# A graph-attention kernel on one core: the work after its last search, laid out in another order and on other engines

## The chip, the core and the metric

The kernel runs on one core of a Trainium2 chip. The core has five engines that each work through their own list of instructions in order: TensorE (PE in the profile; PEld is its loading of weights), VectorE (DVE), ScalarE (ACT), GpSimd (POOL) and SyncE (SP), which here only issues DMAs. They wait for each other by semaphores. 16 DMA engines move data between the chip's memory and the core's own memory. The metric is the time of one execution on the device, in microseconds; lower is better.

## What is computed

The reference is a graph-attention layer with four heads, a residual and a layer norm, over 4096 nodes with 512 features:

```python
ht = (h @ W).reshape(N, N_HEADS, N_HIDDEN).transpose(1, 0, 2)
src = jnp.einsum('hnd,hd->hn', ht, a_src)
dst = jnp.einsum('hnd,hd->hn', ht, a_dst)
e = jax.nn.leaky_relu(src[:, :, None] + dst[:, None, :], SLOPE) + adj_mat[None]
att = jax.nn.softmax(e, axis=-1)
h_prime = jnp.einsum('hij,hjd->hid', att, ht)
return h_prime.mean(axis=0)
...
x = _layernorm(x + _L0_gnn_ref(x, adj, L0_gnn_W, L0_gnn_a), axis=-1)
```

The matrix `adj` (4096 x 4096, 64 MB in fp32) holds values up to 1e9, so in nearly every row one entry is so much larger than all others that the softmax is 1 there and 0 elsewhere. The output row is then the layer norm of x plus one row of x times the mean of W over the heads. The kernel computes this, and tests for every row that the gap to the second largest entry is large enough; where it is not, a general path (a branch that is not taken with these inputs) computes the row in full.

## The kernel before

The 4096 rows are worked on in 32 blocks of 128 (`NB` = 32, row p*32 + ib belongs to block ib). `hold` is a tile with all x rows, block by block; a block's result is written over it and stored from there. The numbers that the text uses: `LATE` = 28 (the last four blocks), `BEHIND` = 24 (the four before them), `Q` = 4, `KB` = 4 pieces of 128 along the 512 features.

The main loop (L400 to L441) takes one block t of `adj` in each pass, while earlier blocks are at later stages:

- `load_adj(t + 5)` issues the DMA of a later block on SyncE; for blocks 28 to 31 in four pieces.
- `segment_maxima` (L158, VectorE) reduces each row's 4096 entries to 64 maxima of segments of 64.
- `find_segment(t)` finds the largest segment (VectorE), computes its address (GpSimd, `row`), and gathers that segment by an indirect DMA that GpSimd issues (`lead`).
- `find_column(t - 2)` finds the place in the segment (VectorE, `within`), computes the column (GpSimd, `col`) and gathers that row of x (`y`, an indirect DMA of GpSimd).
- `turn(t - 3)` transposes the gathered rows on TensorE (4 transposes) and copies the result out of PSUM on ScalarE (`yt`). `residual` starts a PSUM tile with x by a product with the identity, and `products` adds yt times the mean of W, two matmuls for each of four kb (L221).
- `stats(t - 4)` sums and squares the block on ScalarE, `rstd` makes the factor on GpSimd, and `finish` normalises on ScalarE (L261). `row_norm` (L228) sums the squares of x for the test.

Blocks 24 to 27 have no place for their x until then: the rows of `hold` from 16 on held W first, and x of 24 to 31 is loaded only after the last of `adj`. Their products leave PSUM by `put_by` (L234, a ScalarE copy into a free buffer), and x is added later by `add_x` (L237, VectorE).

The last block is searched over its whole row of 4096 (`find_column_in_row`, L201), so that its column is known without a second gather. After the loop comes the drain (L443 to L492), an order written out by hand: every engine takes its instructions in the order of these lines. In it are the x loads of blocks 24 to 31, twelve stores of blocks 0 to 23, the last searches, the row norms, the adding, statistics and normalising of blocks 24 to 31, the test with its three parts (`bound`: the maximum of the row norms, turned by TensorE to one partition, reduced, and spread again by a matmul; `test`: six small VectorE operations; `count`: a matmul that counts, and `report`), and the last stores. Blocks 28 to 30 go through `finish_last` (VectorE adds x to the products, takes `bn_stats` and `bn_aggr`, ScalarE the square root, VectorE the reciprocal and the normalising), block 31 through `finish_in_halves`, the same on two PSUM tiles of 256 columns; `rstd_late` makes the factors of blocks 26 and 27 on VectorE and ScalarE.

PSUM tiles named `o` come from four buffers in turn, tiles `y` from four, `yt` from two.

Of the kernel before, what the change touches and what calls it, by code (L numbers as in the profile page):

```python
# [13 lines left out]
OP = mybir.AluOpType  # L14
# [52 lines left out]
def leading_rows(ctx, tc, x, adj, W, a, out, ident, v, n_bad, any_bad):  # L67
# [47 lines left out]
    def load_x(lo, n):  # L115
        nc.sync.dma_start(hold[:, ds(lo, n), :], x_rows[:, ds(lo, n), :])
# [46 lines left out]
    def find_segment(ib):  # L163
        seg = seg_of.pop(ib)
        nc.vector.max(out=top[:, ib, :], in_=seg)
        at = small.tile([P, 8], U32, name="at")
        nc.vector.max_index(at, top[:, ib, :], seg)  # L167
        row = small.tile([P, 1], U32, name="row")
        nc.gpsimd.tensor_tensor(row, at[:, 0:1], first[:, ib : ib + 1], op=OP.add)  # L169
        lead = small.tile([P, E], F32, name="lead", bufs=2 * Q + 1)  # L170
        nc.gpsimd.indirect_dma_start(  # L171
            out=lead, out_offset=None, in_=adj_segs,
            in_offset=bass.IndirectOffsetOnAxis(ap=row[:, :1], axis=0),
        )
        start = at_of[ib] = small.tile([P, 1], U32, name="start")
        nc.gpsimd.tensor_tensor(start, at[:, 0:1], width, op=OP.mult)
        lead_of[ib] = lead
# [8 lines left out]
    def find_inner(ib):  # L186
        nc.vector.max(out=inner[:, ib, :], in_=lead_of[ib])

    def find_column(ib):
        if ib < BEHIND:  # L190
            find_inner(ib)
        within = small.tile([P, 8], U32, name="within")
        nc.vector.max_index(within, top[:, ib, :], lead_of[ib])  # L193
        col = small.tile([P, 1], U32, name="col")
        nc.gpsimd.tensor_tensor(col, at_of.pop(ib), within[:, 0:1], op=OP.add)  # L195
        gather_rows(ib, col)

    def find_column_in_row(ib):

        col = small.tile([P, 8], U32, name="col")  # L200
        nc.vector.max_index(col, top[:, ib, :], adj_t[ib])  # L201
        gather_rows(ib, col)

    def turn(ib):
        y = y_t.pop(ib)
        tp = psum.tile([P, KB, P], F32, name="tp", bufs=2)
        for kb in range(KB):
            nc.tensor.transpose(tp[:, kb, :], y[:, ts(kb, P)], ident)  # L208
        yt = yt_of[ib] = rows.tile([P, KB, P], F32, name="yt")
        nc.scalar.copy(yt, tp)  # L210
# [5 lines left out]
    def products(ib, lo=0, hi=KB):  # L216
        start = ib not in o_ps
        if start:
            o_ps[ib] = psum.tile([P, D], F32, name="o")
        for kb in range(lo, hi):  # L220
            nc.tensor.matmul(  # L221
                o_ps[ib], yt_of[ib][:, kb, :], w_sum[:, kb, :],
                start=(start and kb == 0), stop=(kb == KB - 1),
            )

    def row_norm(ib):
        sq = rows.tile([P, D], F32, name="sq")
        nc.scalar.activation(sq, hold[:, ib, :], AF.Square, accum_out=xx[:, ib : ib + 1])  # L228
# [4 lines left out]
            o_ps["by"] = adj_pool.tile([P, N // D, D], F32, name="adj_t")  # L233
        nc.scalar.copy(o_ps["by"][:, ib - BEHIND, :], o_ps.pop(ib))  # L234

    def add_x(ib):
        nc.vector.tensor_add(hold[:, ib, :], hold[:, ib, :], o_ps["by"][:, ib - BEHIND, :])  # L237
        o_ps[ib] = hold[:, ib, :]

    def stats(ib):  # L240
# [6 lines left out]
    def rstd(i):  # L247
        nc.gpsimd.tensor_scalar(sd[:, i], sd[:, i], 1.0 / D, EPS, op0=OP.mult, op1=OP.add)
        nc.gpsimd.tensor_tensor(sd[:, i], sd[:, i], power[:, : i.stop - i.start], op=OP.pow)
        nc.gpsimd.tensor_mul(nm[:, i], nm[:, i], sd[:, i])  # L250

    def rstd_late(i):

        nc.vector.tensor_scalar(sd[:, i], sd[:, i], 1.0 / D, EPS, op0=OP.mult, op1=OP.add)
        nc.scalar.activation(sd[:, i], sd[:, i], AF.Sqrt)
        nc.vector.reciprocal(sd[:, i], sd[:, i])
        nc.vector.tensor_mul(nm[:, i], nm[:, i], sd[:, i])

    def finish(ib):
        i = slice(ib, ib + 1)  # L260
        nc.scalar.activation(hold[:, ib, :], o_ps.pop(ib), AF.Identity, bias=nm[:, i], scale=sd[:, i])  # L261
# [10 lines left out]
                start=False, stop=(kb == KB - 1),  # L272
            )

    def finish_in_halves(ib):
        halves = o_ps.pop(ib)
        st = small.tile([P, 2, nc.vector.BN_STATS_DIM], F32, name="st2", bufs=1)
        for k in range(2):
            nc.vector.bn_stats(st[:, k, :], halves[k])
        mv = small.tile([P, nc.vector.BN_AGGR_DIM], F32, name="mv", bufs=2)  # L280
        nc.vector.bn_aggr(mv, st)
        r = small.tile([P, 1], F32, name="r", bufs=2)
        nc.scalar.activation(r, mv[:, 1:2], AF.Sqrt, bias=eps)
        nc.vector.reciprocal(r, r)
        for k in range(2):
            nc.vector.tensor_scalar(
                hold[:, ib, ts(k, D // 2)], halves[k], mv[:, 0:1], r, op0=OP.subtract, op1=OP.mult
            )

    def finish_last(ib, residual):  # L290

        o = o_ps.pop(ib)
        if residual:
            nc.vector.tensor_add(hold[:, ib, :], o, hold[:, ib, :])
            o = hold[:, ib, :]
        st = small.tile([P, nc.vector.BN_STATS_DIM], F32, name="st", bufs=2)
        nc.vector.bn_stats(st, o)
        mv = small.tile([P, nc.vector.BN_AGGR_DIM], F32, name="mv", bufs=2)
        nc.vector.bn_aggr(mv, st)
        r = small.tile([P, 1], F32, name="r", bufs=2)  # L300
        nc.scalar.activation(r, mv[:, 1:2], AF.Sqrt, bias=eps)
        nc.vector.reciprocal(r, r)
        nc.vector.tensor_scalar(hold[:, ib, :], o, mv[:, 0:1], r, op0=OP.subtract, op1=OP.mult)

    def store(queue, lo, n):
        queue.dma_start(out_rows[:, ds(lo, n), :], hold[:, ds(lo, n), :])
# [93 lines left out]
    for t in range(NB):  # L400
        if t == NB // 2:
            tc.mark_branch_hint_location("general", engines=HINTED)
        if t in x_at:
            load_x(*x_at[t])
        load_adj(t + AHEAD)
        middle = 1 if t > LATE else 2
        segment_maxima(t, 0, middle)
        if t >= COLUMN:
            find_column(t - COLUMN)
        segment_maxima(t, middle, PIECES)  # L410
        pair = FINISH <= t < BEHIND + FINISH and t % 2 == 0
        if pair:
            rstd(slice(t - FINISH, t - FINISH + 2))
        find_segment(t)
        if t < 2:
            mean_of_heads(t)
        elif t == 2:
            mean_of_heads(2)
            mean_of_heads(3)
        if t == 0:  # L420
            turn_a()
        turned = [(*vectors[0], turn_w(*vectors.pop(0))) for _ in range(vectors_at.get(t, 0))]
        if t == 16:
            head_norms()
        ib = t - PROJECT
        if ib >= 0:
            turn(ib)
            if ib < BEHIND:
                residual(ib)
        for some in turned:  # L430
            head_vector(*some)
        if ib >= 0:
            products(ib)
        if t >= BEHIND + STATS:
            put_by(t - STATS)
        elif t >= STATS:
            stats(t - STATS)
            row_norm(t - STATS)
        if pair:
            finish(t - FINISH)  # L440
            finish(t - FINISH + 1)  # L441

    for ib in range(BEHIND, NB, 2):  # L443
        load_x(ib, 2)
    for ib in range(0, BEHIND, 2):
        store(nc.sync, ib, 2)
    find_column(NB - 2)
    find_column_in_row(NB - 1)
    for ib in range(BEHIND, NB - 2):
        row_norm(ib)  # L450
    turn(NB - 3)
    for ib in range(NB - 2, NB):
        row_norm(ib)
    products(NB - 3, 0, KB - 1)
    finish_last(NB - 4, True)
    bound(0)
    turn(NB - 2)
    add_x(BEHIND)
    add_x(BEHIND + 1)
    products(NB - 3, KB - 1, KB)  # L460
    residual_in_halves(NB - 1)
    products(NB - 2, 0, 1)
    bound(1)
    products(NB - 2, 1, KB - 1)
    add_x(BEHIND + 2)
    add_x(BEHIND + 3)
    stats(BEHIND)
    stats(BEHIND + 1)
    rstd(slice(BEHIND, BEHIND + 2))
    for ib in range(BEHIND, NB):  # L470
        find_inner(ib)
    bound(2)
    test()
    pg = count()
    stats(BEHIND + 2)
    turn(NB - 1)
    finish_last(NB - 3, True)
    report(pg)
    finish(BEHIND)
    finish(BEHIND + 1)  # L480
    stats(BEHIND + 3)
    products(NB - 2, KB - 1, KB)
    products_of_half(NB - 1, 0)
    products_of_half(NB - 1, 1)
    rstd_late(slice(BEHIND + 2, LATE))
    finish_last(NB - 2, True)
    finish(BEHIND + 2)
    finish(BEHIND + 3)
    for ib, n in ((NB - 4, 1), (NB - 3, 1), (BEHIND, 2), (NB - 2, 1), (BEHIND + 2, 2)):
        store(nc.sync, ib, n)  # L490
    finish_in_halves(NB - 1)
    store(nc.sync, NB - 1, 1)  # L492


# [151 lines left out]
```

## Time and profile before

| | |
|---|---|
| time, median of 5 runs | 245.47 us (243.63 to 245.83) |
| time of the profiled execution | 244.77 us |
| span of the profiled execution, first to last instruction | 243.2 us |
| PE busy | 199.5 us, 82% |
| DVE busy | 189.1 us, 78% |
| ACT busy | 112.2 us, 46% |
| POOL busy | 95.9 us, 39% |
| DMA moved | 97.73 MB, 402 GB/s on average |

Busy time is an average over the whole span. What counts for the end is which wait ends last in the drain, so the profile is read there in order of time. The two lines of the page's DMA part show how the bytes divide, between DMAs that SyncE issues (q1) and the gathers that GpSimd issues (q0); columns are packets, MB and the share of 16 engines' span:

```profile
q1 hardware_dynamic: 11376, 88.09, 87.6%
q0 software_dynamic: 3584, 9.44, 9.9%
```

### The profile page before, as it was taken

To read this page: it belongs to the slowest core of one execution; us is meant where nothing else is said; L and a number is where in the kernel's file an instruction comes from. 1 tells how busy PE (TensorE), PEld (TensorE's weight loads), DVE (VectorE), ACT (ScalarE), POOL (GpSimd) and SP (SyncE) were. 2 spreads that over 40 slices of the span, in tenths; PEclk is the share of its full clock that TensorE was granted. 3 is DMA by queue.
4 is the path that set the end of the run, shared out by engine and by line. 5 is a ranking of instruction groups with operands and counts; after the bars stand their busy time and mean duration, and the time that the engine had idled before them with its cause. 6 is when DMAs were issued, how large, how long until landed. Compare 5 with 4: busy or idle time off the path is not lost.

```text
span 243.2 us, 2510 instructions
## 1 busy us (share of the span) xinstructions
PE 199.5 (82%) x679; PEld 102.9 (42%) x679; DVE 189.1 (78%) x312; ACT 112.2 (46%) x270; POOL 95.9 (39%) x209
## 2 busy tenths in 40 slices
PE   0098959999999999999959779499959888769950
PEld 0034515655555555555324334144424444324530
DVE  2625885499789886999589969895999999986753
ACT  2003002155757575757636455238533851364961
POOL 1012232426435542645254636463556474441100
PEclk9999778999999999999999999979997999997996
DMA  6999999999999999999999999999999999999944
GB/s 238 416 414 424 422 424 426 418 428 412 424 418 421 411 442 413 424 412 430 424 417 416 429 420 424 408 425 424 428 418 398 408 406 409 407 407 418 409 186 175
DMA packets 14993, 97.73 MB, mean 402 GB/s; under 512 B 2296, under 2 KB 2296, under 8 KB 10240
## 3 DMA queue, kind: packets, MB, share of 16 engines
q1 hardware_dynamic: 11376, 88.09, 87.6%
q0 software_dynamic: 3584, 9.44, 9.9%
q8 instruction: 6, 0.10, 0.2%
q14 instruction: 11, 0.09, 0.1%
q10 hardware_dynamic: 16, 0.02, 0.0%
HBM read 89.15 MB, written 8.39 MB: 401 GB/s over the span
## 4 chain that ended last, share of the span: by engine, by line


## 5 line engine op out<-in xcount | busy, mean ns | idle before, releaser
L158 DVE TENSOR_REDUCE seg<-adj_t 128x32 f32<-128x2048 f32 (+1 forms) x74 | 146.3, 1987 | 37.5 <-DMA adj_t<-in_adj_dram 37.3
L221 PE MATMUL o<-w_sum,yt 128*128 128x512 f32 x248 | 118.6, 620 | 4.2 <-ACT yt L210 4.2
L221 PEld LDWEIGHTS o<-w_sum,yt 128*128 128x128 f32 x248 | 46.4, 197 | 59.2 <-issue 45.8
L210 ACT COPY yt<-tp 128x512 f32<-128x512 f32 x32 | 18.8, 587 | 51.4 <-PE tp L208 51.4
L171 POOL DMA_INDIRECT lead<-in_adj_dram,row x32 | 32.2, 1006 | 14.3 <-POOL row L169 14.3
L181 POOL DMA_INDIRECT y<-in_x_dram,col x32 | 30.7, 961 | 17.8 <-POOL col L195 14.9
L311 PE MATMUL o<-hold,ident 128*128 128x512 f32 x32 | 21.1, 821 | 15.5 <-DMA hold<-in_L_gnn_W_dram 15.5
L208 PE MATMUL tp<-ident,y 128*128 128x128 f32 x128 | 19.6, 276 | 11.9 <-DMA y<-in_x_dram,col 11.6
L214 PE MATMUL o<-hold,ident 128*128 128x512 f32 x48 | 25.5, 614 | 0.0
L208 PEld LDWEIGHTS tp<-ident,y 128*128 128x128 f32 x128 | 14.6, 141 | 24.3 <-issue 23.5
L195 POOL TENSOR_TENSOR col<-start,within 128x1 uint32<-128x1 uint32 x31 | 5.8, 188 | 47.0 <-DVE within L193 46.8
L329 ACT COPY wt<-tp 128x512 f32<-128x512 f32 x16 | 9.2, 587 | 31.6 <-PE tp L327 31.6
L169 POOL TENSOR_TENSOR row<-at,first 128x1 uint32<-128x1 uint32 x32 | 6.0, 188 | 41.5 <-DVE at L167 41.5
L228 ACT ACTIVATE sq<-hold 128x512 f32<-128x512 f32 x32 | 19.8, 620 | 0.0
L335 PEld LDWEIGHTS pv<-at_d,wt 128*128 128x128 f32 x128 | 16.3, 191 | 6.8 <-ACT wt L329 3.5
L311 PEld LDWEIGHTS o<-hold,ident 128*128 128x128 f32 x32 | 8.0, 262 | 26.1 <-POOL row L169 11.7
L312 ACT ACTIVATE w_sum<-o 128x512 f32<-128x512 f32 x4 | 2.4, 598 | 34.0 <-PE o L311 34.0
L261 ACT ACTIVATE hold<-o,nm,sd 128x512 f32<-128x512 f32 x24 | 17.2, 770 | 0.0
L245 ACT ACTIVATE sq<-o,nm 128x512 f32<-128x512 f32 x24 | 16.5, 687 | 0.8
L335 PE MATMUL pv<-at_d,wt 128*128 128x2 f32 x128 | 15.3, 244 | 0.6 <-ACT wt L329 0.6
L243 ACT ACTIVATE sq<-o 128x512 f32<-128x512 f32 x24 | 14.6, 608 | 0.0
L327 PEld LDWEIGHTS tp<-ident,hold 128*128 128x128 f32 x64 | 7.9, 142 | 6.9 <-issue 6.9
(87 smaller groups left out, 135.1 us busy)
## 6 DMA issues: line engine op xcount, KB each, us to landing
adj_t<-in_adj_dram SPq DMA_DIRECT2D x27, 2048.0 KB, 32.0
adj_t<-in_adj_dram SPq DMA_DIRECT2D x20, 512.0 KB, 12.0
out_dram<-hold SPq DMA_DIRECT2D x14, 512.0 KB, 12.0
hold<-in_x_dram SPq DMA_DIRECT2D x6, 1024.0 KB, 33.7
hold<-in_L_gnn_W_dram SPq DMA_DIRECT2D x4, 1024.0 KB, 18.0
hold<-in_x_dram SPq DMA_DIRECT2D x4, 512.0 KB, 12.1
out_dram<-hold SPq DMA_DIRECT2D x4, 256.0 KB, 3.2
lead<-in_adj_dram,row POOLq DMA_INDIRECT x32, 6.2
```

Of the source, the lines that this page charges most:

```text
L158: nc.vector.tensor_reduce(seg_of[ib][:, ts(k, S // n)], adj_t[ib][:, ts(k, N // n)].rearrange("p (s e) -> p s e", e=E), axis=AX.X, op=OP.max,)
L171: nc.gpsimd.indirect_dma_start(out=lead, out_offset=None, in_=adj_segs, in_offset=bass.IndirectOffsetOnAxis(ap=row[:, :1], axis=0),)
L181: nc.gpsimd.indirect_dma_start(out=y, out_offset=None, in_=x, in_offset=bass.IndirectOffsetOnAxis(ap=col[:, :1], axis=0),)
L208: nc.tensor.transpose(tp[:, kb, :], y[:, ts(kb, P)], ident)
L210: nc.scalar.copy(yt, tp)
L214: nc.tensor.matmul(o_ps[ib], ident, hold[:, ib, :], start=True, stop=False)
L221: nc.tensor.matmul(o_ps[ib], yt_of[ib][:, kb, :], w_sum[:, kb, :], start=(start and kb == 0), stop=(kb == KB - 1),)
L228: nc.scalar.activation(sq, hold[:, ib, :], AF.Square, accum_out=xx[:, ib : ib + 1])
L245: nc.scalar.activation(sq, o, AF.Square, bias=nm[:, i], accum_out=sd[:, i])
L261: nc.scalar.activation(hold[:, ib, :], o_ps.pop(ib), AF.Identity, bias=nm[:, i], scale=sd[:, i])
L311: nc.tensor.matmul(o, ident, hold[:, w_at + kb * H + h, :], start=(h == 0), stop=(h == H - 1))
L335: nc.tensor.matmul(pv[:, kb, h : 2 * H : H], wt[:, k, :], at_d[:, k, h : 2 * H : H], start=(k == 0), stop=(k == KB - 1),)
```

## The change

Four things are altered. The products of blocks 24 and later are split: the first three kb come in the block's own pass, the last one after the next block's transposes. x is added to blocks 28 and 29 by a `residual` matmul and to blocks 24, 25 and 26 by GpSimd, which takes the place of VectorE (block 27 stays there). Block 27's statistics move from ScalarE to VectorE (`moments`, `factor`), with the normalising still on ScalarE; blocks 28 and 29 are normalised straight from PSUM. The last block's second half is normalised on ScalarE beside the first half on VectorE, and its two `bn_stats` are issued apart. The x loads of the last blocks are issued in another order (24, 28, 26, 30), the first two early stores are one, and the steps of the test stand at other places among the rest.

```diff
@@ -233,8 +233,8 @@
             o_ps["by"] = adj_pool.tile([P, N // D, D], F32, name="adj_t")
         nc.scalar.copy(o_ps["by"][:, ib - BEHIND, :], o_ps.pop(ib))

-    def add_x(ib):
-        nc.vector.tensor_add(hold[:, ib, :], hold[:, ib, :], o_ps["by"][:, ib - BEHIND, :])
+    def add_x(engine, ib):
+        engine.tensor_add(hold[:, ib, :], hold[:, ib, :], o_ps["by"][:, ib - BEHIND, :])
         o_ps[ib] = hold[:, ib, :]

     def stats(ib):
@@ -249,13 +249,6 @@
         nc.gpsimd.tensor_tensor(sd[:, i], sd[:, i], power[:, : i.stop - i.start], op=OP.pow)
         nc.gpsimd.tensor_mul(nm[:, i], nm[:, i], sd[:, i])

-    def rstd_late(i):
-
-        nc.vector.tensor_scalar(sd[:, i], sd[:, i], 1.0 / D, EPS, op0=OP.mult, op1=OP.add)
-        nc.scalar.activation(sd[:, i], sd[:, i], AF.Sqrt)
-        nc.vector.reciprocal(sd[:, i], sd[:, i])
-        nc.vector.tensor_mul(nm[:, i], nm[:, i], sd[:, i])
-
     def finish(ib):
         i = slice(ib, ib + 1)
         nc.scalar.activation(hold[:, ib, :], o_ps.pop(ib), AF.Identity, bias=nm[:, i], scale=sd[:, i])
@@ -272,35 +265,42 @@
                 start=False, stop=(kb == KB - 1),
             )

+    mean_var, rt = {}, {}
+
+    def moments(ib):
+
+        if ib < NB - 1:
+            st = small.tile([P, nc.vector.BN_STATS_DIM], F32, name="st", bufs=2)
+            nc.vector.bn_stats(st, o_ps[ib])
+        else:
+            st = halves_st
+        mv = mean_var[ib] = small.tile([P, nc.vector.BN_AGGR_DIM], F32, name="mv", bufs=3)
+        nc.vector.bn_aggr(mv, st)
+        r = rt[ib] = sd[:, ib : ib + 1]
+        nc.scalar.activation(r, mv[:, 1:2], AF.Sqrt, bias=eps)
+
+    def factor(ib, shift=False):
+        nc.vector.reciprocal(rt[ib], rt[ib])
+        if shift:
+            nc.vector.scalar_tensor_tensor(
+                nm[:, ib : ib + 1], mean_var[ib][:, 0:1], -1.0, rt[ib], op0=OP.mult, op1=OP.mult
+            )
+
+    def normalise(ib, o, columns=slice(0, D)):
+        nc.vector.tensor_scalar(
+            hold[:, ib, columns], o, mean_var[ib][:, 0:1], rt[ib], op0=OP.subtract, op1=OP.mult
+        )
+
+    halves_st = once.tile([P, 2, nc.vector.BN_STATS_DIM], F32, name="halves_st")
+
+    def stats_of_half(ib, k):
+        nc.vector.bn_stats(halves_st[:, k, :], o_ps[ib][k])
+
     def finish_in_halves(ib):
-        halves = o_ps.pop(ib)
-        st = small.tile([P, 2, nc.vector.BN_STATS_DIM], F32, name="st2", bufs=1)
-        for k in range(2):
-            nc.vector.bn_stats(st[:, k, :], halves[k])
-        mv = small.tile([P, nc.vector.BN_AGGR_DIM], F32, name="mv", bufs=2)
-        nc.vector.bn_aggr(mv, st)
-        r = small.tile([P, 1], F32, name="r", bufs=2)
-        nc.scalar.activation(r, mv[:, 1:2], AF.Sqrt, bias=eps)
-        nc.vector.reciprocal(r, r)
-        for k in range(2):
-            nc.vector.tensor_scalar(
-                hold[:, ib, ts(k, D // 2)], halves[k], mv[:, 0:1], r, op0=OP.subtract, op1=OP.mult
-            )
-
-    def finish_last(ib, residual):
-
-        o = o_ps.pop(ib)
-        if residual:
-            nc.vector.tensor_add(hold[:, ib, :], o, hold[:, ib, :])
-            o = hold[:, ib, :]
-        st = small.tile([P, nc.vector.BN_STATS_DIM], F32, name="st", bufs=2)
-        nc.vector.bn_stats(st, o)
-        mv = small.tile([P, nc.vector.BN_AGGR_DIM], F32, name="mv", bufs=2)
-        nc.vector.bn_aggr(mv, st)
-        r = small.tile([P, 1], F32, name="r", bufs=2)
-        nc.scalar.activation(r, mv[:, 1:2], AF.Sqrt, bias=eps)
-        nc.vector.reciprocal(r, r)
-        nc.vector.tensor_scalar(hold[:, ib, :], o, mv[:, 0:1], r, op0=OP.subtract, op1=OP.mult)
+
+        halves, i = o_ps.pop(ib), slice(ib, ib + 1)
+        normalise(ib, halves[0], slice(0, D // 2))
+        nc.scalar.activation(hold[:, ib, D // 2 :], halves[1], AF.Identity, bias=nm[:, i], scale=sd[:, i])

     def store(queue, lo, n):
         queue.dma_start(out_rows[:, ds(lo, n), :], hold[:, ds(lo, n), :])
@@ -411,6 +411,12 @@
         pair = FINISH <= t < BEHIND + FINISH and t % 2 == 0
         if pair:
             rstd(slice(t - FINISH, t - FINISH + 2))
+        if t == NB - 1:
+            for ib in (BEHIND, LATE, BEHIND + 2, LATE + 2):
+                load_x(ib, 2)
+            row_norm(BEHIND)
+            row_norm(BEHIND + 1)
+            add_x(nc.gpsimd, BEHIND)
         find_segment(t)
         if t < 2:
             mean_of_heads(t)
@@ -425,12 +431,14 @@
         ib = t - PROJECT
         if ib >= 0:
             turn(ib)
-            if ib < BEHIND:
+            if ib > BEHIND:
+                products(ib - 1, KB - 1, KB)
+            if ib < BEHIND or ib == LATE:
                 residual(ib)
         for some in turned:
             head_vector(*some)
         if ib >= 0:
-            products(ib)
+            products(ib, 0, KB if ib < BEHIND else KB - 1)
         if t >= BEHIND + STATS:
             put_by(t - STATS)
         elif t >= STATS:
@@ -440,55 +448,68 @@
             finish(t - FINISH)
             finish(t - FINISH + 1)

-    for ib in range(BEHIND, NB, 2):
-        load_x(ib, 2)
-    for ib in range(0, BEHIND, 2):
+    row_norm(BEHIND + 2)
+    row_norm(BEHIND + 3)
+    row_norm(LATE)
+    store(nc.sync, 0, Q)
+    for ib in range(Q, BEHIND, 2):
         store(nc.sync, ib, 2)
     find_column(NB - 2)
+    add_x(nc.gpsimd, BEHIND + 1)
     find_column_in_row(NB - 1)
-    for ib in range(BEHIND, NB - 2):
+    add_x(nc.gpsimd, BEHIND + 2)
+    turn(NB - 3)
+    products(NB - 4, KB - 1, KB)
+    residual(NB - 3)
+    products(NB - 3)
+    for ib in range(LATE + 1, NB):
         row_norm(ib)
-    turn(NB - 3)
-    for ib in range(NB - 2, NB):
-        row_norm(ib)
-    products(NB - 3, 0, KB - 1)
-    finish_last(NB - 4, True)
+    stats(BEHIND)
+    moments(LATE)
     bound(0)
+    for ib in range(BEHIND, NB):
+        find_inner(ib)
+    factor(LATE)
+    normalise(LATE, o_ps.pop(LATE))
     turn(NB - 2)
-    add_x(BEHIND)
-    add_x(BEHIND + 1)
-    products(NB - 3, KB - 1, KB)
     residual_in_halves(NB - 1)
     products(NB - 2, 0, 1)
     bound(1)
+    add_x(nc.vector, LATE - 1)
+    stats(BEHIND + 1)
+    moments(LATE - 1)
     products(NB - 2, 1, KB - 1)
-    add_x(BEHIND + 2)
-    add_x(BEHIND + 3)
-    stats(BEHIND)
-    stats(BEHIND + 1)
     rstd(slice(BEHIND, BEHIND + 2))
-    for ib in range(BEHIND, NB):
-        find_inner(ib)
+    stats(BEHIND + 2)
     bound(2)
     test()
     pg = count()
-    stats(BEHIND + 2)
+    rstd(slice(BEHIND + 2, BEHIND + 3))
+    moments(NB - 3)
+    factor(LATE - 1, shift=True)
+    report(pg)
+    factor(NB - 3)
+    normalise(NB - 3, o_ps.pop(NB - 3))
     turn(NB - 1)
-    finish_last(NB - 3, True)
-    report(pg)
     finish(BEHIND)
     finish(BEHIND + 1)
-    stats(BEHIND + 3)
     products(NB - 2, KB - 1, KB)
     products_of_half(NB - 1, 0)
     products_of_half(NB - 1, 1)
-    rstd_late(slice(BEHIND + 2, LATE))
-    finish_last(NB - 2, True)
+    nc.vector.tensor_add(hold[:, NB - 2, :], o_ps[NB - 2], hold[:, NB - 2, :])
+    o_ps[NB - 2] = hold[:, NB - 2, :]
+    moments(NB - 2)
+    stats_of_half(NB - 1, 0)
+    factor(NB - 2)
+    normalise(NB - 2, o_ps.pop(NB - 2))
     finish(BEHIND + 2)
     finish(BEHIND + 3)
+    stats_of_half(NB - 1, 1)
+    moments(NB - 1)
+    factor(NB - 1, shift=True)
+    finish_in_halves(NB - 1)
     for ib, n in ((NB - 4, 1), (NB - 3, 1), (BEHIND, 2), (NB - 2, 1), (BEHIND + 2, 2)):
         store(nc.sync, ib, n)
-    finish_in_halves(NB - 1)
     store(nc.sync, NB - 1, 1)


```

## The prediction

> **What bounds the kernel now.** I read the page's slices first, then the list of instructions in order of time from 190 us on, then windows of 1 us there, then SyncE's queue.
>
> The slices (tenths of busy time, 6.08 us each):
>
> ```profile
> PEclk9999778999999999999999999979997999997996
> DMA  6999999999999999999999999999999999999944
> ```
>
> For 38 slices the DMA engines are full: the stream of adj (64 MB) sets the pace, and nothing here shortens it. Only the last two slices have room. The change lies there, so I take the tail alone. TensorE in order of time (start, duration, engine, line, operation; in brackets idle time and what ended it):
>
> ```profile
> 212.64 3.70 PE L221 MATMUL o<-w_sum,yt 128*128 128x512 f32 x8 [0.73 <-ACT yt L210]
> 218.03 0.63 PE L208 MATMUL tp<-ident,y 128*128 128x128 f32 x4 [1.69 <-DMA y<-in_x_dram,col]
> 219.33 4.39 PE L221 MATMUL o<-w_sum,yt 128*128 128x512 f32 x6 [0.67 <-ACT yt L210]
> ...
> 229.00 0.22 PE L386 MATMUL px<-gap,ones 128*1 128x32 f32 x2
> ...
> 230.51 3.70 PE L270 MATMUL o<-w_sum,yt 128*128 128x256 f32 x16
> ```
>
> TensorE stops at 216.34, waits for block 29's gathered rows until 218.03, and then has no pause over 0.7 us up to its last matmul at 234.2. Six matmuls at 219.33 take 4.39 us; eight at 212.64 took 3.70. The windows say why (columns: stretch, length, busy time of PE, PEld, DVE, ACT, POOL, then granted clock, DMA share, GB/s):
>
> ```profile
> 219.00:220.00 1.00, 0.67 (x1) 0.50 (x2) 0.88 (x2) 1.00 (x4) 0.83 (x1) 0.54 1.00 410
> 220.00:221.00 1.00, 1.00 (x2) 0.33 (x1) 0.24 (x2) 0.69 (x3) 0.11 (x1) 0.50 1.05 422
> 221.00:222.00 1.00, 1.00 (x2) 0.33 (x1) 1.00 (x3) 0.00 (x0) 0.00 (x0) 0.50 1.00 401
> 222.00:223.00 1.00, 1.00 (x3) 0.52 (x2) 0.76 (x2) 0.00 (x0) 0.00 (x0) 0.76 1.04 426
> ```
>
> The clock is halved from about 219.1 to 222.5, 3.4 us, which loses 1.7 us of matmul time. The other engines, in order of time:
>
> ```profile
> 213.99 4.42 DVE L201 FIND_INDEX8 col<-top,adj_t 128x8 uint32<-128x4096 f32 x1
> ...
> 219.17 0.94 POOL L181 DMA_INDIRECT y<-in_x_dram,col  x1 [2.95 <-PE tp L208]
> ...
> 233.52 0.17 DVE L254 TENSOR_SCALAR sd<-sd 128x2 f32<-128x2 f32 x1 [1.76 <-ACT sq L245]
> ...
> 234.24 0.69 DVE L294 TENSOR_TENSOR hold<-o,hold 128x512 f32<-128x512 f32 x1
> ...
> 238.46 0.99 DVE L286 TENSOR_SCALAR hold<-o,mv,r 128x256 f32<-128x256 f32 x2
> ```
>
> This is the loss: VectorE stands idle from 231.76 until ScalarE has block 27's statistics at 233.5, and only then adds block 30 (whose products ended at 230.67). So 5.25 us pass between the last matmul (234.2) and the last result (239.45). SyncE's queue:
>
> ```profile
> 237.01 0.96 SPq L306 DMA_DIRECT2D out_dram<-hold  x2
> 239.48 0.33 SPq L306 DMA_DIRECT2D out_dram<-hold  x1
> ```
>
> The last store goes out at 239.48, the span ends 3.7 us later (243.2), and the profiled run's time is 244.77, 1.57 more.
>
> **The change part by part.** I lay the new order out by hand with this trace's durations. A 128x512 fp32 matmul starts every 0.43 us, a kb is two.
>
> *Late products* (kb 3 of block ib after turn(ib+1)). Work on TensorE is the same; the 0.7 us wait for each yt copy is filled. Before t=31 that is worth nothing: the DVE period (5.35 us between searches) and the gathers set the pace. put_by comes about 0.5 us later on ScalarE, which idles 2 to 4 us there.
>
> *residual(28) and residual(29) on TensorE*, 2 matmuls = 0.86 us each, replacing two VectorE adds of 0.68. residual(28) waits for x 28-29, now the second x load: issued 201.22, 11.7 us to landing, so 212.9; queued behind it are products(28), which then run 213.8 to 216.6. Before they ended at 216.34, and block 29's rows still come at 218.0. Cost nothing; the cover is 1.4 us. If that load came at 216, 1.7 us of it would reach the end.
>
> *row_norm(24), (25) before yt(28) on ScalarE.* Their x lands at 199.33 + 12.3 = 211.6; two norms at 0.62 put yt(28) at 212.95 to 213.5, before products(28) at 213.8. Nothing.
>
> *Three adds on GpSimd.* The nearest row:
>
> ```profile
> masks.py:199 POOL TENSOR_SCALAR_AFFINE_SELECT ident<-ident 128x128 f32<-128x128 f32 x1 | 0.3, 291 | 0.1
> ```
>
> Against 0.19 for 128x1 that is 0.1 us per 128 columns, so 0.6 us for 512 columns of one input and about 1.0 for two. [...] I take 1.2, ends 0.6 and 2.5. add_x(24) runs 211.6 to 212.9, ahead of row(31), lead(31) and y30's gather, and row(31) came at 212.97 anyway. add_x(25), after y30's gather, runs 216.2 to 217.4; y31's gather waits for the search (218.4) regardless. add_x(26) runs after it. [...] At 2.5 us each y30 would come 0.8 later, still covered. VectorE saves three adds, 1.9 us.
>
> *The clock.* Ordinary matmuls paused 216.34 to 219.33, 3.0 us with only transposes inside, and the clock halved. At 142.91 there was a pause of 1.68 and transposes, some 2.2 us in all, and it stayed at 1.00. Now products(28,3) follow turn(29) at once: the pause is 216.6 to 218.5, 1.9 us. [...] The trace shows 3.0 was enough, so I go by it: 1.9 stays at full clock, worth 1.7 us.
>
> *TensorE from 218.03 on.* turn(29) 0.45, products(28,3) 0.86, residual(29) 0.86, products(29) 3.44, xm's transpose 0.11: 223.75. turn(30) 0.45, residual of 31's halves 0.86: 225.1. Block 30 takes block 28's PSUM buffer, so it needs normalise(28): o28 219.6, statistics 220.5, its square root behind row_norm(31) and stats(24) at 222.9, done 223.8; no stall. yt(30) is copied at 225.5, a stall of 0.45. products(30,0) and the broadcast 1.26: 226.8; two kb 1.9: 228.7. count needs test: the broadcast at 226.5, plus what it took before (2.2 to count): 228.7. turn(31) and products(30,3) 1.5: 230.2 (y31 landed by about 227). Halves 3.7: last matmul 233.9, against 234.2. So 1.7 us of clock pay for 1.7 us of residual and late product.
>
> *The finish.* stats(27) leaves ScalarE, its add and bn_stats go to VectorE at 224.2 to 225.7, where VectorE waits for the broadcast. VectorE after test (228.25): block 29's statistics 0.9, factor(27) 0.35, report 0.45, factor and normalise(29) 0.95: 231.0. Block 30's add, statistics and the first half's bn_stats 2.0: 233.0; factor and normalise 0.75: 233.75, just before the last matmul. Then second half 0.4, bn_aggr 0.24, square root 0.33, reciprocal 0.2, shift 0.2, half a normalise 0.55 (two took 0.99): 1.95. ScalarE's half, estimated at 0.58 from the 0.80 of 512 columns, ends beside it. Last store at 236.0 instead of 239.48. The others go out at 231, 232, 233.6 and 234.4: 1.8 MB at 410 GB/s from 231.3, when the early stores are through, need 4.4 us, so DMA doesn't hold the last one. In SyncE's queue the x loads keep their place behind adj, only their order changes, and one early store of 1 MB for two of 0.5 moves the same bytes. GpSimd's rstd(26) (1.1 us by 0.19, 0.72 and 0.20 of block 24's) runs at about 229, long before finish(26), and frees VectorE and ScalarE of rstd_late.
>
> Sum: 3.5 us off 244.77, 241.3. That execution lies 0.7 below the median of the five runs shown (245.47), so for a median I say 242.0.
>
> **The rivals.**
> - *The clock halves anyway*, or VectorE, with only 0.2 us of room before the last half, is late by as much. [...] Against: 142.91. TensorE ends 1.7 later, at 235.6: 243.7. Chance 0.22.
> - *The finish slips further* (ScalarE's small steps behind 1.4 us statistics, stores queued behind finish(26), (27)): 3 us of the gain lost, 245.0. Against: no step's input is over 1 us late in my layout. 0.11.
> - *GpSimd's adds are very slow*, and y30's gather stands behind add_x(24). Place: turn(30). From 211.6, an add of over about 6 us puts block 30's rows 3.5 us late and all gain is gone; at 9 us the time is 248.5. [...] With other waits of the kind, 0.08.
> - *It doesn't do what it says*: if TensorE can't fill the wait for yt, another 0.7 us, inside the second case.
>
> **How the numbers follow.** The forecast has 0.59, at 242.0, give or take 1.3. The five runs spread over 2.2 us, so about 1% (2.5 us) is what can be told from no change: under 243.0 counts as faster. Forecast 0.53 of its 0.59, first rival 0.04: faster 0.57. Slower 0.08, the rest 0.35. Range 240.6 to 244.5: the forecast with its error, and the halved clock.
>
> **What would show it.** Right: granted clock 1.00 from 216 to 234; last matmul near 234; no wait of VectorE on ScalarE's statistics; last store near 236; GpSimd's add near 1.2 us. Wrong: a 0.50 clock after 219, y30's gather after 216.5, a search (L201) longer than 4.42, or bn_stats of the second half starting over 0.3 us after the last matmul.

## The result, and the profile after

| | before | changed |
|---|---|---|
| time, median | 244.12 us (51 runs) | 242.69 us (30 runs) |
| ratio, 95% interval | | 0.9935 [0.9921, 0.9950] |
| profiled execution: time, span | 244.77, 243.2 us | 242.43, 240.9 us |

The changed kernel is 1.4 us faster by the medians (0.65% by the ratio), less than half of the 3.5 us that were forecast. Its time is 0.7 us from the forecast of 242.0 and in the range. That it comes so near is luck: the gain is 2.1 us too small, and in the larger sample the kernel before has a median 1.35 us below the 245.47 of the five runs, so that two misses offset each other.

The slices of the changed kernel:

```profile
PEclk9999797999999999999999999999997999999996
DMA  6999999999999999999999999999999999999995
```

After its 31st slice (187 us) the clock row has no dip until the last one, where TensorE has finished; DMA now works at half its capacity even in that slice. The instructions of the changed kernel in order of time, columns as in the prediction:

```profile
213.61 0.23 DVE L165 MAX8 top<-seg 128x8 f32<-128x64 f32 x1
...
214.00 1.27 POOL L237 TENSOR_TENSOR hold<-hold,adj_t 128x512 f32<-128x512 f32 x1 [1.78 <-ACT sq L228]
...
218.77 0.63 PE L208 MATMUL tp<-ident,y 128*128 128x128 f32 x4 [0.53 <-DMA y<-in_x_dram,col]
219.23 1.02 PE L221 MATMUL o<-w_sum,yt 128*128 128x512 f32 x2
...
225.30 0.63 PE L208 MATMUL tp<-ident,y 128*128 128x128 f32 x4 [0.64 <-DMA y<-in_x_dram,col]
...
231.38 3.70 PE L263 MATMUL o<-w_sum,yt 128*128 128x256 f32 x16
...
235.12 0.43 DVE L297 BATCH_NORM_STATS2 halves_st<-o 128x6 f32<-128x256 f32 x1 [0.65 <-PE o L263]
...
236.43 0.54 DVE L290 TENSOR_SCALAR hold<-o,mv,sd 128x256 f32<-128x256 f32 x1
236.55 0.56 ACT L303 ACTIVATE hold<-o,nm,sd 128x256 f32<-128x256 f32 x1 [0.43 <-DVE nm L285]
...
237.14 0.33 SPq L306 DMA_DIRECT2D out_dram<-hold  x1
```

Read it from the bottom. The last matmul ends at 235.08 and the last store goes out at 237.14: 2.06 us, where the kernel before needed 5.27. VectorE waits for TensorE there (`<-PE o L263`) and no longer for ScalarE's statistics. So the finish does what it was made for. But 3.2 us were saved there, and these two executions are only 2.3 us apart in span (the medians only 1.4, since the profiled 244.77 lies 0.65 us above its median and 242.43 lies 0.26 below). The first row says where to look: VectorE has the last block's segment maxima at 213.61. In the kernel before the same instruction stands at

```profile
212.26 0.23 DVE L165 MAX8 top<-seg 128x8 f32<-128x64 f32 x1
```

That is 1.35 us earlier. The block's adj loads were issued long before anything that the change rearranges in the drain. The loss of these 1.35 us lies in the stream, which the prediction had set aside.

### The profile page after: what moved, and what is told of

Its sections match the earlier page's. It is cut to its first block, busy times and chain, and to the rows that moved or that the text cites. A ratio compares the mean times of both kernels' runs of the same rounds, so it can differ in the third digit from the quotient of the medians.

```text
span 240.9 us, 2519 instructions
## 1 busy us (share of the span) xinstructions
PE 197.2 (82%) x683; PEld 101.0 (42%) x683; DVE 186.8 (78%) x308; ACT 111.6 (46%) x267; POOL 100.9 (42%) x215
## 2 busy tenths in 40 slices
DMA packets 14849, 97.73 MB, mean 406 GB/s; under 512 B 2280, under 2 KB 2280, under 8 KB 9968
## 3 DMA queue, kind: packets, MB, share of 16 engines
q1 hardware_dynamic: 11232, 88.09, 88.9%
## 4 chain that ended last, share of the span: by engine, by line
issue 35%; POOL 33%; DMA 21%; PE 4%; DVE 4%; POOLq 1%; SPq 1%; ACT 0%; DVEq 0%
DMA adj_t<-in_adj_dram 15%; POOL lead L171 11%; POOL y L181 10%; POOL sd L249 4%; DMA y<-in_x_dram,col 3%; DMA lead<-in_adj_dram,row 2%; POOL start L176 2%; POOL row L169 2%; POOL col L195 2%; DVE seg L158 2%; PE o L221 2%; PE o L263 1%; POOL sd L248 1%; POOL nm L250 1%; DVE col L201 1%
## 5 line engine op out<-in xcount | busy, mean ns | idle before, releaser
L221 PE MATMUL o<-w_sum,yt 128*128 128x512 f32 x248 | 115.9, 608 | 0.7 <-ACT yt L210 0.7
L221 PEld LDWEIGHTS o<-w_sum,yt 128*128 128x128 f32 x248 | 44.9, 192 | 53.9 <-issue 42.8
```

The lines of the kernel that those rows point to most:

```text
L221: nc.tensor.matmul(o_ps[ib], yt_of[ib][:, kb, :], w_sum[:, kb, :], start=(start and kb == 0), stop=(kb == KB - 1),)
```

## The experiments

Three theories were to be told apart. A: something in the drain takes the gain back (a wait behind GpSimd's add, the late products, the order of the finish). B: DMA is the bound, with 97.73 MB to move, and finishing earlier only piles up the stores. C, formed after the first two groups: the change moved the tiles to other addresses, and the stream is slower for that.

**The same kernels again.** No edit.

> The changed kernel, unaltered, profiled and timed again. Theory A: the last search starts anywhere from 214.0 to 215.5, since the code of the loop is the same up to block 27, and the drain takes about 21 us again. Rival B: the last search starts near 215.4 again, 1.4 later than in before. Ratio to before about 0.994 in both.

> The kernel before, profiled a second time. Theory A (the profiled execution of before was dearer than the usual one, because the clock halved for 3.4 us in its drain): here the granted clock stays at 1.00 from 216 us on, the time from the end of the last search to the end of the span is about 23.3 us instead of 24.8, and the span is near 242.4. Rival B (the usual drain is the one seen, and the new kernel loses 1.4 us in the loop because of the change): the clock halves again, the drain takes 24.8 us, and the last search starts near 214.0.

The changed kernel: 242.60 us, 0.9927 [0.9901, 0.9953], segment maxima at 213.30. The kernel before: one time, 243.87, span 242.3 us, segment maxima at 212.09. So the late stream comes back. A lowered clock comes back too, but at another place: in this execution of the kernel before it lies earlier, in the 36th slice (212.0 to 218.1 us, 0.7 in the clock row). From TensorE in order of time:

```profile
213.63 5.26 PE L221 MATMUL o<-w_sum,yt 128*128 128x512 f32 x8 [0.73 <-ACT yt L210]
```

Eight matmuls take 5.26 us in place of 3.70, but ahead of the wait for block 29's rows, where little of it reaches the end: from the segment maxima to the last matmul it is 21.24 us, against 21.95 in the execution that the prediction was built on.

**GpSimd's add of block 24 behind y30's gather.** In the changed kernel that add waits 1.78 us for ScalarE (`row_norm(24)` reads the same rows of `hold` that the add overwrites), and y30's gather queues behind it; TensorE then waits 0.64 us for the rows.

```diff
-            add_x(nc.gpsimd, BEHIND)          # at t == NB - 1
...
     find_column(NB - 2)
+    add_x(nc.gpsimd, BEHIND)
```

> GpSimd adds x to block 24 after it has issued block 30's gather instead of before. Theory: add_x(24) had to wait for row_norm(24), which reads what it overwrites, so block 30's gather went out 0.7 us late and its transposes waited 0.64 us; that wait goes, the last matmul comes about 0.6 us after-to-after earlier and the time falls by 0.4 to 0.6 us against the changed kernel. Rival (the stores bind the end, or count's wait takes its place): no change within 0.2 us.

242.53 us, 0.9935 [0.9911, 0.9959]: the same. The wait is real and was not foreseen: behind the add, y30's gather goes out 3.68 us after the segment maxima, and 3.00 with the add moved. TensorE's wait for the rows falls from 0.64 to 0.27 us, but in the second profile of the changed kernel there is none at all. It is not what sets the end.

**Block 27 back on ScalarE**, in the places that it had before:

```diff
-    moments(LATE - 1)
-    rstd(slice(BEHIND + 2, BEHIND + 3))
-    factor(LATE - 1, shift=True)
...
+    stats(BEHIND + 3)                  # after finish(BEHIND + 1)
...
+    rstd_late(slice(BEHIND + 2, LATE)) # ahead of block 30's add
```

> The changed kernel with block 27's statistics back on ScalarE, after finish(24) and finish(25), and the factors of 26 and 27 by VectorE and ScalarE as before; everything else as changed. Theory: this was the largest part of the gain: VectorE waits for ScalarE again, until about 235.3, and the last result comes some 2.5 to 3 us later than in the changed kernel, so slower than before by 1 us. Rival (the half on ScalarE and the clock carry the gain): under 1 us slower than the changed kernel.

244.94 us, 1.0027 [1.0007, 1.0048]: the whole gain is gone, and a little more, 2.3 us above the changed kernel. VectorE in order of time:

```profile
234.68 0.17 DVE L253 TENSOR_SCALAR sd<-sd 128x2 f32<-128x2 f32 x1 [2.63 <-ACT sq L245]
```

It stands idle for 2.63 us, until 234.68, for the same reason as in the kernel before (1.76 us there). So moving this block is what the finish lives on. And with it undone the rest of the change is a loss, which again asks for a cost elsewhere.

**1 MB of stores left out**, in both kernels. Blocks 0 to 3 (changed kernel: `store(nc.sync, 0, Q)`; before: the loop of stores begins at 4) are not written.

```diff
-    store(nc.sync, 0, Q)
```

> The changed kernel without the store of blocks 0 to 3, which leaves 1 MB of the output unwritten (2.5 us of DMA at 410 GB/s), all behind the stream of adj. Theory C (in the changed kernel the DMA engines, full until 237 us, now end last, and hold back the last store): its time falls by 0.7 to 1.5 us, and the span ends 3.7 us after the last store is issued, as in before, instead of 4.5. Rival (the chain of TensorE and VectorE still ends last, and DMA only seems full): under 0.3 us.

> The same store of blocks 0 to 3 left out of the kernel before (1 MB unwritten). Theory C: here DMA had idle time at 235 to 237 us, so the time stays within 0.4 us. Rival (fewer stores also land block 31's and 30's gathered rows sooner, and this is what helps): it falls by as much as in the changed kernel.

At the 406 GB/s of the changed kernel's page 1 MB is 2.6 us of transfer. The changed kernel fell to 241.97 us, 0.9899 [0.9852, 0.9947], 0.7 below its 242.69, with overlapping intervals from six runs; the kernel before did not move (244.12, 0.9993 [0.9967, 1.0020]). So theory B explains at most that 0.7; with a megabyte less, something else ends last. In the changed kernel DMA is nevertheless close behind. Windows at its end (columns as in the prediction):

```profile
232.00:234.00 2.00, 2.00 (x11) 1.77 (x10) 1.77 (x6) 1.41 (x4) 0.00 (x0) 1.00 0.92 356
234.00:236.00 2.00, 1.08 (x6) 0.60 (x4) 1.11 (x3) 1.18 (x3) 0.00 (x0) 1.00 0.91 350
236.00:238.00 2.00, 0.00 (x0) 0.00 (x0) 0.78 (x3) 0.69 (x2) 0.00 (x0) 0.80 0.79 316
```

The stores keep DMA at 0.8 to 0.9 until the last of them has been issued; there is no slack of several microseconds, only of some tenths.

**The place of `halves_st`.** The changed kernel keeps its statistics of halves in a tile of the lasting pool, ahead of `adj_t` in memory, and so moves the adj buffers. Here it lies in the pool of small tiles, and the adj buffers are back where they were.

```diff
-    halves_st = once.tile([P, 2, nc.vector.BN_STATS_DIM], F32, name="halves_st")
+    halves_st = small.tile([P, 2, nc.vector.BN_STATS_DIM], F32, name="halves_st", bufs=1)
```

> The changed kernel with the small tile halves_st taken from another pool, so that the six adj buffers lie at the same place in the core's memory as in before (64 bytes lower). Theory D (the stream of adj runs about 1.3 us slower in the changed kernel because its buffers were moved): the last search starts near 214.3 instead of 215.1 to 216.3, and the time falls by about 1 us. Rival (the later search in four profiles was chance): within 0.3 us of the changed kernel, search near 215.

242.72 us, 0.9921 [0.9892, 0.9950], segment maxima at 214.62. It is not the adj buffers' address. This profile shows another thing: here, with the changed kernel's order of work, the clock was lowered in the drain as well (0.7 in the slice from 211.8 to 217.9 us). The clock rows of this profile and of the second one of the kernel before, both with a dip in their 36th slice:

```profile
PEclk9999799999999999999998999999797999979999
```

```profile
PEclk9999799599999999999999999999999999979995
```

**ScalarE's half of block 31 back on VectorE.**

```diff
-        nc.scalar.activation(hold[:, ib, D // 2 :], halves[1], AF.Identity, bias=nm[:, i], scale=sd[:, i])
+        normalise(ib, halves[1], slice(D // 2, D))
...
-    factor(NB - 1, shift=True)
+    factor(NB - 1)
```

> The changed kernel with both halves of block 31 normalised on VectorE, one after the other. Theory: the last result comes 0.35 us later (0.99 for two halves, against 0.68 from the shift operation to ScalarE's end), of which the full DMA engines may hide a part: 0.1 to 0.4 us slower than the changed kernel. Rival (the end is bound by DMA alone): no change.

243.21 us, 0.9959 [0.9939, 0.9979]: 0.5 above the changed kernel, with intervals that overlap, so a cost of this half alone is not shown by the times. From the last matmul to the last store it took 2.29 us, 0.23 more.

**The gathered rows at a multiple of 64 bytes.** What else moves with the change are the tiles of the last pool, `y`, `yt`, `sq` and `wt`: by the sizes of the small tiles (`st2` and `r` go, `mv` gets a third buffer, `halves_st` comes) `y` starts at byte 204000 of each partition and not at 204032. That is 32 bytes past a multiple of 64, where it was a multiple before. These are the places in the programs built from the kernels. A small tile that nothing uses puts it back; one in the kernel before takes it away.

```diff
+    small.tile([P, 8], F32, name="pad", bufs=1)
```

> The changed kernel with 32 unused bytes put into the pool of small tiles, so that the gathered rows of x (tiles y) and the tiles behind them begin at a multiple of 64 bytes, as in before; in the changed kernel they begin 32 bytes beside one, because the small tiles were changed. Theory E (the gathers write y into the core's memory at a worse place, and this takes 0.4 us per 8 blocks from the stream of adj): the stretch from the search of block 12 to that of block 20 takes 50.4 us instead of 50.7 to 51.0, the last block's segments are found near 212.3 instead of 213.3 to 214.6, and the time falls by 0.7 to 1.3 us against the changed kernel, to about 241.6. Rival (something else, or chance, makes the stream slower): the stretch stays at 50.7 or more and the time within 0.3 us of 242.6.

> The kernel before with the same 32 bytes, which there move y off the multiple of 64. Theory E: its stretch from block 12 to 20 becomes 50.7 or more instead of 50.3 to 50.5, the last segments are found after 213.2, and it is 0.7 to 1.3 us slower than before. Rival: as before in both.

This makes the difference. The changed kernel with the unused tile: 240.48 us (six runs), 0.9853 [0.9817, 0.9888], an interval that does not meet the changed kernel's own. That is 2.1 us less, more than the 0.7 to 1.3 expected; by the intervals it could be 0.8 to 3.2. The kernel before with the tile: 245.50 us, 1.0062 [1.0036, 1.0088]. One window over the stream, from 50 us to 212, shows it for all four (the last number is GB/s). Before:

```profile
50.00:212.00 162.00, 146.40 (x502) 74.34 (x500) 141.34 (x220) 87.72 (x211) 79.94 (x168) 0.98 1.01 418
```

The kernel before with `y` moved off:

```profile
50.00:212.00 162.00, 145.24 (x496) 73.71 (x494) 140.67 (x219) 87.37 (x211) 79.64 (x168) 0.98 1.01 414
```

The changed kernel:

```profile
50.00:212.00 162.00, 143.34 (x494) 71.85 (x492) 140.69 (x219) 87.53 (x211) 79.75 (x168) 0.99 1.01 415
```

The changed kernel with `y` put back:

```profile
50.00:212.00 162.00, 145.90 (x500) 73.42 (x498) 141.97 (x221) 88.23 (x213) 80.26 (x168) 0.98 1.01 419
```

DMA is full in all four (the share 1.01), but moves 1% less in the same time, and 1% of 162 us is 1.6 us. The same window gives 418 or 419 GB/s in all five profiles with `y` in place, and 414 or 415 in six of the nine without. The last block's segment maxima follow. With `y` off in the kernel before, and with `y` back in the changed one:

```profile
213.69 0.23 DVE L166 MAX8 top<-seg 128x8 f32<-128x64 f32 x1
```

```profile
211.95 0.23 DVE L165 MAX8 top<-seg 128x8 f32<-128x64 f32 x1
```

Over all profiles they come between 211.66 and 212.26 in the five with `y` at a multiple of 64, and between 213.30 and 214.62 in the nine without; none lies between. `lead`, the other tile that gathers write, is excluded by the pair: the unused tile moves it too, onto a multiple in both kernels, and one became faster and the other slower. What is not separated is whether it is the gathers' writes into `y`, or `yt`, `sq` and `wt`, which lie in the same pool and move along. That a full DMA moves less would fit the gathers. But the longer time is not in the gathers' own packets: they take 10.0% of the 16 engines' span in the changed kernel, with `y` back too, some 24 us both times. Those of SyncE's queue take 88.9% of 240.9 us, and with `y` back 88.9% of 238.9, which is 1.8 us less. So the mechanism is open.

Nor is 64 shown to be the step that counts. The only multiple of 64 that was run for `y`, 204032, is a multiple of 256 as well; the other two places, 204000 and 204064, lie 32 bytes to either side of it. And it is no rule for every target of a DMA: `adj` and `hold` start 32 bytes past a multiple of 64 in both kernels. Only the last experiment puts them on one, and its stream runs at the same 419 GB/s as with the last pool alone.

**The late products undone**: all four kb of a block directly after its turn.

```diff
-            if ib > BEHIND:
-                products(ib - 1, KB - 1, KB)
...
-            products(ib, 0, KB if ib < BEHIND else KB - 1)
+            products(ib)
...
-    products(NB - 4, KB - 1, KB)
```

> The changed kernel with all four products of a block in its own pass, so that TensorE waits for each yt copy again. Theory: the pause of the ordinary matmuls before block 29 grows from about 2.2 to some 2.8 us, TensorE waits 0.65 us more for yt(29), but has 0.86 us less to do behind turn(29); the last matmul comes within 0.4 us of the changed kernel's, and the time within 0.3 us, unless the clock halves at 219, which would cost up to 1.7. Rival (the late products carry the gain): slower than the changed kernel by 1 us or more.

242.38 us, 0.9934 [0.9914, 0.9954]: the same as with them. The last matmul comes even sooner, at 233.45, although the stream was among the later ones (214.09), and the last store goes out at 235.50; then 5.30 us pass to the end of the span, where the changed kernel has 3.76. Its last matmuls, and a window behind the last store:

```profile
229.75 3.70 PE L263 MATMUL o<-w_sum,yt 128*128 128x256 f32 x16
```

```profile
236.00:238.00 2.00, 0.00 (x0) 0.00 (x0) 0.00 (x0) 0.00 (x0) 0.00 (x0) 0.80 0.83 329
```

No engine computes there, and DMA is still 83% busy with stores: here the stores themselves are the end. Taken with the megabyte left out, this says that with `y` off its place two ends lie close together, that of computing and that of the stores. Computing that ends 1.6 us earlier gains nothing clear of noise, and less to store gains at most 0.7. A faster stream brings both forward, which fits its larger gain. So theory B was in part right.

**All at once**: `adj`, `hold`, `lead` and the last pool on a multiple of 64, block 24's add behind y30's gather, block 29's residual ahead of its turn, and the count of the test with its `report` moved behind later work.

```diff
+    keep.tile([P, 8], F32, name="pad0")
...
-            add_x(nc.gpsimd, BEHIND)
...
+    add_x(nc.gpsimd, BEHIND)      # after find_column(NB - 2)
...
+    residual(NB - 3)              # ahead of turn(NB - 3)
...
-    residual(NB - 3)
...
-    pg = count()
...
-    report(pg)
...
+    pg = count()          # after products(NB - 2, KB - 1, KB)
...
+    report(pg)            # after stats_of_half(NB - 1, 0)
```

> The changed kernel with add_x(24) behind block 30's gather, residual(29) ahead of turn(29), count behind block 30's last product and report behind the first half's statistics, and 32 bytes put ahead of all tiles, so that adj, hold, lead and y all begin at a multiple of 64 bytes. Theories C and E together: with the stream not slowed, the last matmul comes 1 to 2 us earlier than in the changed kernel, but the DMA engines end last, so the time is that of y_aligned or up to 0.5 us less: 241.0 to 241.7. Rival (where the tiles lie does nothing): 242.3 to 242.7, as the DMA engines hold the end.

242.43 us, 0.9923 [0.9893, 0.9953]: no gain over the changed kernel, although the last matmul ends at 232.06 and the last store goes out at 234.12, the earliest of all. Windows of its end:

```profile
234.00:236.00 2.00, 0.00 (x0) 0.00 (x0) 0.00 (x0) 0.09 (x1) 0.00 (x0) 0.75 0.87 335
236.00:238.00 2.00, 0.00 (x0) 0.00 (x0) 0.00 (x0) 0.00 (x0) 0.00 (x0) 0.50 0.13 49
238.00:240.00 2.00, 0.00 (x0) 0.00 (x0) 0.00 (x0) 0.00 (x0) 0.00 (x0) 0.50 0.00 0
```

From 236 us on no engine computes and next to nothing moves. GpSimd's queue (duration min/median/max in ns, first and last start) is what runs, at the line of the branch and at the program's last line:

```profile
L63 POOLq INC_SWDGE_SEM  x1: 1472/1472/1472, 232.7 to 232.7; - x1
```

```profile
L663 POOLq DRAIN  x3: 44/103/5306, 234.2 to 240.0; - x3
```

The program branches on the flag that `report` makes. With `report` late the flag is there at 231.15; the branch is at 231.8, then come 1.47 and 5.31 us that only GpSimd spends, and the end at 240.3, 9.15 us after the flag. The two take as long elsewhere: the first 1.48 us in the kernel before and in the changed one, the drain 5.31 in these two, their second profiles and the one with `y` back. But there the report comes early enough for the stores to end later. Moving it behind other work has made it the end. The fastest version found is the changed kernel with the unused tile, 240.48 us.

## Why the prediction was right and wrong

- *The finish* was right: 1.95 us and 2.1 for the store were laid out, 2.06 measured. Block 27's move carries it (2.63 us of waiting come back when it is undone).
- *The layout of TensorE* was right as a length. From the segment maxima (212.26) to the last matmul (233.9) it had 21.6 us; the changed kernel took 21.47 and 21.00, with `y` back 21.17. The waits inside were others. The prediction had GpSimd's add run from 211.6 without asking who reads the rows that it overwrites; it waited 1.78 us, and y30's gather went out at 217.29. That is after the 216.5 named as a sign of being wrong: 1.35 us of it is the stream, 0.7 the add.
- *GpSimd's add*: the row of the trace gave about 1.0 us for two inputs. The 1.2 of the layout, and its dearer end of 2.5, go beyond that as the author's estimate, and no run shows them; in their place the three adds of the changed kernel took 1.27 to 1.28 us each, and VectorE's search, with the second of them beside it, kept its 4.42 us.
- *The clock* stayed at full speed in the drain of the changed kernel's profile, as said (1.00 in every window of 1 us from 187 to 237), and from 200 us to the last matmul in three of its variants (`y` back, the late products undone, all at once); in the one with `halves_st` among the small tiles it was lowered (0.7 in the 36th slice). But the length of the pause, 3.0 us, by which the prediction went did not decide it alone: in the second profile of the kernel before the ordinary matmuls had paused for 2.7 us ahead of the eight that took 5.26 us, and in the one with the tile added they paused for 3.2 us at full clock (1.00 from 217 to 221 us). What decides it, no run shows. And its worth was read off one execution. Of two more profiles of the kernel before, the one with the tile added has 1.00 from 200 to 239 us, the other has the low clock where it costs little, and from the segment maxima to the last matmul they take 20.66 and 21.24 us, not 21.95. So the 1.7 us that were to pay for the late products and residuals on TensorE were mostly not there to be won.
- *The late products*: the sum had them fill the wait for yt and take time in the drain that the clock would pay for. Undone, TensorE needs 19.36 us from the segment maxima to the last matmul, not 21.47 or 21.00, in one profile, and the time stays. So they cost up to 2 us of TensorE's time there, 0.86 of it by the layout's own figure, which the stores hide; where the rest comes from was not worked out.
- *DMA*: "DMA doesn't hold the last one" was too sure. From last store to end of span it took 3.76 and 4.74 us in two profiles of the changed kernel, and 5.30 where computing ended sooner; by this measure the stores decide up to a microsecond in the changed kernel.
- *The step that failed* is the first: "The change lies there, so I take the tail alone", with the stream as something that "nothing here shortens". The change also resized small tiles, and with them shifted the last pool, with the gathered rows, by 32 bytes. That made the stream 1.3 to 1.7 us later and took about 2 of the 3.5 us back: with only this put back, the time is 3.76 us below its runs of the kernel before (244.24), close to the forecast's 3.5.

The agreement of 3.76 with 3.5 is partly luck, since most of the clock's share of the forecast was not there in two more profiles of the kernel before. What remains open: which tile of the last pool it is, by what mechanism, and whether 64, 128 or 256 is the multiple that counts; how much the stores still hold when `y` is in place; and whether the late products or an earlier report would matter then. None of these was run.

## What to carry to other kernels

When a change adds, drops or resizes even a small tile, look at whether the tiles behind it, the targets of gathers among them, have moved against multiples of 64 bytes or more (32 bytes off one went with 1.3 and 2.1 us here); compare a window of the code that was not changed before explaining anything in the code that was. Size a clock effect from several executions, since it may be in one and not in the next. And before moving a flag that the program branches on, count what the engines still have to do after the branch.

## What the runs showed of the hardware

- With the pool of the gathered rows and their neighbours moved 32 bytes off a multiple of 64 (and of 256), the stream from 50 to 212 us ran at 414 or 415 GB/s and not at 418 or 419, at the same DMA share of 1.01, in six profiles against five; the time was 1.26 us longer in the kernel before, about 2.1 in the changed one. The same offset of `adj` and `hold` did not slow it: 419 GB/s with it (`y` back) and without it (all at once).
- After its last branch GpSimd needed 1.47 us for one instruction of its queue (1.48 in the kernel before and the changed one) and 5.31 for a drain. In the last experiment, where nothing else was left to do, the end of the program so lay 9.15 us after the flag.
- The clock was halved for about 3.4 us (0.50 at 220 to 222 us) after a pause of 3.0 us of ordinary matmuls with transposes inside, and in another execution lowered (0.7 from 212.0 to 218.1 us) around the end of one of 2.7 us; a pause of 3.2 us (the kernel before with the tile added), and one of 2.9 in the last experiment, passed at 1.00. The length of the pause alone did not decide it.
